# A transformer block on one core: the place of some products, copies, maxima and one feed-forward half in a written-out order of tasks

## The chip, the cores and the metric

The kernel runs on one core of a Trainium2 chip. The metric is the device time of one execution in microseconds (us), as the median of three runs. One more execution was recorded by the profiler. A core has these engines, each of which runs its own queue of instructions in order: TensorE (PE, with its weight loads shown apart as PEld), VectorE (DVE), ScalarE (ACT), GpSimd (POOL) and SyncE (SP), which here only starts transfers. An instruction waits until the instructions that it depends on, on whatever engine, are done, and everything behind it on its own engine waits too.

## The reference

The input x has 8 batches of 512 tokens with 128 features. Everything is float32. The computation has three steps:

```python
x = x + 0.5 * ffn(layernorm(x))
x = x + attn(layernorm(x))
x = x + 0.5 * ffn(layernorm(x))
```

```python
# ffn: three blocks, each with two quantized linear layers with a low-rank addition
h = x
for blk in range(3):
    y = qlora_linear(h, 2 * blk)
    y = gelu(layernorm(y) * gamma[blk] + beta[blk])     # exact Gelu
    h = qlora_linear(y, 2 * blk + 1) + h
# attn: 16 heads of rank 64
xq = einsum('btd,hrd->bthr', x, Q)
xk = einsum('bud,hrd->buhr', x, K)
scores = einsum('bthr,buhr->bthu', xq, xk) / sqrt(128)
out = einsum('bthu,bud,hde->bte', softmax(scores), x, VO)
```

## The kernel before

**Attention.** The heads are taken two at a time, so a batch has 8 pairs and the program 64. A pair is laid out over a period of 16 units of an abstract time, that is two halves of 8 units. In each half two of the four chunks of 128 query rows are treated: PE makes the scores of both heads (`scores`, L554), DVE their negated maxima (`maxima`, L570), ACT the exponentials with their sums (`exps`, L573), DVE the inverse of the sums (`inverse`), POOL and ACT the divisions (`divide`, L585: one head on POOL, the other on ACT, or both on POOL in halves listed in `gelu_halves`). DVE transposes blocks of 32 by 32 (`turn`, L592), and 16 transfers started on SP move the blocks between groups of partitions (`exchange`, L603). One period later PE multiplies the result with the values (`attend`, L620, one 512-column product for each head and chunk, summed in one PSUM bank over the 8 pairs of a batch). In the first half of a pair PE also makes the projections of the next pair (`project`, L507) and in the second half the values (`values`, L534), which ACT copies.

**Feed-forward.** One half of the feed-forward (first or last, f = 0 or 1) of one batch is laid out by `lay_ffn` (L449) as a unit in the midst of the attention, up to two units at a time. A unit normalizes its input, and then has three blocks of four halves each: first product (L278), bias and statistics on DVE (L286), root on POOL, scaling on DVE, transpose on PE, Gelu on ACT (L303, with a load of ACT's function table before it and one for the exponentials after it), second product (L312) and sum on DVE (L318). A last transpose and sum go back to x (`ffn_add`, L328). Batch 0's first and batch 7's last feed-forward are laid out by `lay_parts` (L409) at the start and the end of the program, in two parts of 256 tokens each, where nothing runs beside them but the weights' preparation.

**Order.** `at(t, fn, *args)` notes a task with its time. At the end `run_tasks` sorts all tasks by time and then by the order of noting, and calls them. The times are not waited for: they only fix the order of the instructions on each engine, which is kept by dependencies between neighbours. So a change of a time matters where it passes another task with work on the same engine.

**The start.** Abstract time starts at T0 = -33; pair 0 has its first scores at 0. Before that lie the weights' preparation (`Weights`, two groups of layers), the transposes of Q and K by `projection_weights` (L219), each with a copy by ACT, and batch 0's first feed-forward. In halves 0 to 3 no attention products can run yet: this is called the filling. In it, `busy` puts transposes of nothing on PE.

Of the kernel before, what the change touches and what calls it, by code (L numbers as in the profile page):

```python
# [18 lines left out]
def kernel(  # L19
# [25 lines left out]
    nc = tc.nc  # L45
# [8 lines left out]
    NC = T // P  # L54
# [3 lines left out]
    HALF = 8.0  # L58
# [9 lines left out]
    def bank(name, tag="proj"):  # L68
        return psum.tile([P, NC, P], F32, tag=tag, name=name, bufs=1)

    ident = const.tile([P, P], F32, name="ident")
# [57 lines left out]
    def at(t, fn, *args):  # L129
        tasks.append((t, len(tasks), fn, args))  # L130
# [44 lines left out]
    class Weights:  # L175
# [33 lines left out]
        def turn(self):  # L209
            pt = bank(f"pt_w{self.l0}", "proj")  # L210
            for l in range(self.n):
                nc.tensor.transpose(pt[:, l, :], wf[:, self.l0 + l, :], ident)
            nc.scalar.copy(wT[:, self.l0 : self.l1, :], pt[:, : self.n, :])
# [2 lines left out]
    qT_w = const.tile([P, HP, P], F32, name="qT_w")  # L216
    kT_w = const.tile([P, HP, P], F32, name="kT_w")

    def projection_weights(src, dst, g0, scale, nm):  # L219
        pt = bank(f"pt_{nm}{g0}", "proj")  # L220
        for j in range(NC):
            nc.tensor.transpose(pt[:, j, :], src[:, g0 + j, :], ident)
        nc.scalar.mul(dst[:, g0 : g0 + NC, :], pt, scale)

    def transposed(src, name, tag):

# [219 lines left out]

    gelu_halves = set()

    def lay_ffn(units, t0, lead=None):  # L449

        for i, unit in enumerate(units):
            if unit is None:
                continue
            f, b = unit  # L460
            tag = f"f{i}"
            n = Norm(xs[b], f"n{f}_{b}", tag)
            t = t0 + i * HALF
            for at_n, (fn, *args) in zip(
                lead or [t + 6.0] + [t + HALF + dt for dt in (0.5, 2.6, 4.2, 6.5)],
                ((n.stats,), (n.root,), (n.scale,), (n.turn,), (ffn_start, n, f, b)),
            ):
                at(at_n, fn, *args)
            for k in range(NB):
                u = t0 + (2 + 4 * k) * HALF  # L470
                t = u + i * HALF
                m = Block(f, k, b, tag)
                gelu_halves.add(round((u + 2 * HALF) / HALF))
                at(t + 2.3, m.first)
                at(t + 6.0, m.biased)
                at(t + HALF + 0.5, m.root)
                at(u + 2 * HALF + 2.6, m.scale)
                at(u + 2 * HALF + 4.2 + i, m.turn)
                at(u + 2 * HALF + 6.5, m.gelu)
                at(u + 3 * HALF + 2.3 + 1.9 * i, m.second)  # L480
                at(u + 3 * HALF + 6.0, m.add)
            at(t0 + (2 + 4 * NB) * HALF + 2.3 + 1.9 * i, ffn_add, f, b, tag)

# [146 lines left out]
    def attn_add(b):  # L630
        oT = work.tile([P, NC, P], F32, tag="oT", name=f"oT{b}", bufs=2)
        nc.vector.tensor_copy(
            oT.rearrange("p c (i q) -> p i c q", q=32),
            accs[b].rearrange("p (i c q) -> p i c q", i=Q4, q=32),
        )

        def turn():
            po = transposed(oT, f"pot{b}", "f0")
            nc.vector.tensor_tensor(xs[b], xs[b], po, ALU.add)

        return turn
# [18 lines left out]
    def lay_pair(n, b, g):  # L660

        m = Pair(b, g)
        t = n * PERIOD
        if n == 0:
            for i in range(2):
                for (wt, nm), tm, tag in zip(  # L670
                    ((kT_w, "k"), (qT_w, "q")), ((-3.6, -3.5), (-1.1, 0.3))[i],
                    (("proj", "f0"), ("proj", "f1"))[i],
                ):
                    at(tm, m.project_part, wt, nm, i, tag)
        else:
            for i, (wt, nm) in enumerate(((qT_w, "q"), (kT_w, "k"))):
                at(t - PERIOD + 2.5 + 2.7 * i, m.project, wt, nm)
                at(t - PERIOD + 3.9 + 2.3 * i, m.keep, nm)
        for c in range(NC):
            h, i = c // 2, c % 2  # L680
            u = t + h * HALF
            at(u, m.scores, c)
            at(u + 1.2 + 1.3 * i, m.maxima, c)
            at(u + 2.6 + 1.5 * i, m.exps, c)
            at(u + 4.4 + 1.2 * i, m.inverse, c)
            at(u + 4.5 + 1.2 * i, m.divide, c, 0, "pool")
            shared = "pool" if 2 * n + h in gelu_halves else "act"
            at(u + 5.0 + 0.75 * i, m.divide, c, 1, shared)
            at(u + (HALF + 2.7 if i else 6.9), m.turn, c)
        at(t + PERIOD + 2.8, m.exchange)  # L690
        for i in range(2):
            u = t + PERIOD + HALF
            at(u - HALF + 2.4 if m.last else u + 2.5 + 2.7 * i, m.values, 2 * i)
            at(u - HALF + 2.5 if m.last else u + 3.9 + 2.3 * i, m.keep_values, 2 * i)
        for i in range(2 * NC):
            u = t + 2 * PERIOD + i // NC * HALF
            at(u + (3.0, 3.5, 4.0, 5.0)[i % NC], m.attend, i // NC, i % NC)
        if g == HP - 1 and b < B - 1:
            done = []
            at(t + 3 * PERIOD - 0.1, lambda: done.append(attn_add(b)))  # L700
            at(t + 3 * PERIOD + 4.2, lambda: done[0]())
# [5 lines left out]
    T0 = -33.0  # L707
# [3 lines left out]
    at(T0 + 6.0, busy, 4)  # L711
    at(T0 + 9.65, columns)
    for (l0, l1), times in zip(groups, (
        (5.4, 5.5, 6.1, 6.55, 7.3, 7.8), (8.3, 9.0, 10.0, 10.6, 11.9, 12.65)
    )):
        m = Weights(l0, l1)
        for t, fn in zip(
            times, (m.dequantized, m.lora_turn, m.lora_keep, m.lora, m.add, m.turn)
        ):
            at(T0 + t, fn)  # L720
    for t, (src, dst, g0, scale, nm) in zip((17.55, 20.35, 23.05, 26.0), (
        (q_sb, qT_w, 0, 1.0 / math.sqrt(D), "q"), (k_sb, kT_w, 0, 1.0, "k"),
        (q_sb, qT_w, NC, 1.0 / math.sqrt(D), "q"), (k_sb, kT_w, NC, 1.0, "k"),
    )):
        at(T0 + t, projection_weights, src, dst, g0, scale, nm)

    def input_part(m, t):
        def keep():
# [11 lines left out]
        0, 0, [[T0 + t for t in times] for times in (  # L740
            (3.7, 6.4, 7.2, 7.6, 7.5), (4.3, 7.7, 8.2, 8.6, 9.6)
        )],
        T0 + 8.7, 1.4, (2, 2, 2), input_part,
    )
    at(T0 + 27.3, table, AF.Exp)
    for t in (26.6, 28.0, 29.9, 30.8):
# [1 line left out]
    for h in range(4):  # L748
        at((h + 1) * HALF - 0.1, busy, 12)

    lay_ffn([(0, 1)], -2 * HALF, (-3.3, -2.9, -1.6, 0.5, 0.6))
    lay_ffn([None, (0, 2)], 6 * HALF)
    for b in range(B):
        t = b * HP * PERIOD
        if b + 1 < B:
            lay_attn_input(b + 1, t + (4 if b else 12) * HALF)
        if b:
            halves = [(1, b - 1)]
            if b + 2 < B:
                halves.append((0, b + 2))  # L760
            lay_ffn(halves, t + 5 * HALF)
    for n in range(B * HP):
        lay_pair(n, n // HP, n % HP)


    E = (B * HP + 2) * PERIOD

    def store_part(m, t):
# [8 lines left out]
        1, B - 1, [[E + t for t in times] for times in (  # L777
            (1.8, 3.7, 4.2, 4.6, 1.5), (2.8, 4.8, 5.3, 5.7, 1.6)
        )],
        E + 5.0, 1.1, (6, 6, 6), store_part,  # L780
    )
    at(E + 1.65, idle_bank, "acc")
    at(E + 1.7, busy, 18)
# [54 lines left out]
```

## Time and profile before

| | before |
|---|---|
| median of three runs | 1152.51 us (1152.16 to 1153.66) |
| profiled execution | 1156.43 us |
| its span, first to last instruction | 1154.6 us |
| granted TensorE clock, mean | 0.996 |
| PE, DVE, ACT, POOL busy | 96%, 75%, 64%, 50% of the span |
| 16 transfers of each exchange (`eT<-tr`) | 128 KB each, 2.3 us from issue to landing (median) |

A row of the timeline gives start, duration, engine, line, operation, what is written and read, the count, and in brackets the idle time of the engine before it and what ended it. `L314` is line 314 of the kernel. A row of a wait list gives the total in us, the number of times and the longest. A matmul in float32 shows as two records. Small differences between rows come from records that overlap.

### The profile page before, as it was taken

The page shows a single profiled execution, that of the slowest core. Times are in us where ns is not written, and L with a number is a line of the kernel's source. Part 1 is how long each engine was busy: PE and PEld are TensorE (multiplying, and loading weights), DVE is VectorE, ACT ScalarE, POOL GpSimd, SP SyncE. Part 2 cuts the span into 40 slices and gives each one's busy share as a digit, 9 for nine tenths or more (in the row PEclk, how much of TensorE's full clock was granted, in tenths as well). Part 3 has the DMA queues.
Part 4 walks back from the last instruction along what each step waited for, and adds up shares of the span by engine and source line. Part 5 has one row for each costly group of instructions (what it writes and reads, how often), then busy time and mean ns, then how long its engine had stood idle before and what let it go on. Part 6 is the DMA issues. An engine that isn't in the chain of part 4 may idle for free.

```text
span 1154.6 us, 14081 instructions
## 1 busy us (share of the span) xinstructions
PE 1106.9 (96%) x3951; PEld 553.3 (48%) x3951; DVE 862.7 (75%) x1771; ACT 743.0 (64%) x1632; POOL 572.7 (50%) x477
## 2 busy tenths in 40 slices
PE   8789999999999999999999999999999999999997
PEld 6444444445444444444444444444444444444445
DVE  5667777887879777887778787797778777677635
ACT  2567676766666766767666666676666676766731
POOL 2345555554546455455545546454554555545512
PEclk9989999999999999999999999999999999999999
DMA  6055565566546545654655564565465656655550
GB/s 175 1 121 112 132 137 128 112 134 147 117 112 147 130 107 128 142 130 110 139 117 125 133 141 106 128 146 119 107 139 131 139 114 137 150 134 123 129 141 10
DMA packets 57286, 142.29 MB, mean 123 GB/s; under 512 B 18348, under 2 KB 22008, under 8 KB 57208
## 3 DMA queue, kind: packets, MB, share of 16 engines
q1 hardware_dynamic: 54840, 139.73, 53.9%
q10 hardware_dynamic: 2368, 1.66, 0.6%
q8 instruction: 32, 0.52, 0.2%
q14 instruction: 46, 0.38, 0.1%
HBM read 5.01 MB, written 2.10 MB: 6 GB/s over the span
## 4 chain that ended last, share of the span: by engine, by line
PE 84%; ACT 7%; DVE 4%; SPq 2%; DMA 1%; issue 1%; POOL 1%; ACTq 0%; DVEq 0%
PE acc L624 36%; PE ps L564 16%; PE pv L544 9%; PE pq L510 5%; PE pk L510 4%; PE py L281 4%; PE po L314 4%; ACT L306 3%; SPq L613 2%; ACT aT L306 2%; PE p L230 2%; DVE tr L598 1%; ACT v L550 1%; DVE nm L571 1%; DMA eT<-tr 1%
## 5 line engine op out<-in xcount | busy, mean ns | idle before, releaser
L588 POOL TENSOR_SCALAR e<-e,rden 128x512 f32<-128x512 f32 x306 | 476.1, 1568 | 510.0 <-DVE rden L583 510.0
L576 ACT ACTIVATE e<-ps,nm 128x512 f32<-128x512 f32 x512 | 349.5, 692 | 197.6 <-DVE nm L571 195.3
L624 PE MATMUL acc<-eT,v 128*128 128x512 f32 x1024 | 471.6, 593 | 3.2 <-DMA eT<-tr 1.7
L598 DVE STREAM_TRANSPOSE tr<-e 128x1024 f32<-128x1024 f32 x256 | 315.6, 1233 | 107.4 <-POOL e L588 103.3
L571 DVE TENSOR_REDUCE nm<-ps 128x2 f32<-128x1024 f32 x256 | 299.3, 1206 | 18.9 <-PE ps L564 17.5
L624 PEld LDWEIGHTS acc<-eT,v 128*128 128x128 f32 x1024 | 189.9, 190 | 200.3 <-issue 189.5
L564 PE MATMUL ps<-k,q 64*128 64x512 f32 x1024 | 254.9, 616 | 1.9 <-ACT e L576 1.5
L564 PEld LDWEIGHTS ps<-k,q 64*128 64x128 f32 x1024 | 88.2, 186 | 130.1 <-issue 79.2
L590 ACT ACTIVATE e<-e,rden 128x512 f32<-128x512 f32 x206 | 138.2, 728 | 7.1 <-DVE rden L583 6.8
L544 PE MATMUL pv<-vo_sb,axT 128*128 128x256 f32 x512 | 135.6, 388 | 4.4 <-ACT v L550 4.4
L550 ACT COPY v<-pv 128x512 f32<-128x512 f32 x128 | 74.6, 583 | 76.3 <-PE pv L544 75.9
L583 DVE RECIPROCAL rden<-den 128x2 f32<-128x2 f32 x256 | 36.0, 148 | 113.2 <-ACT e L576 111.9
L544 PEld LDWEIGHTS pv<-vo_sb,axT 128*128 128x128 f32 x512 | 91.6, 191 | 58.8 <-issue 35.6
L576 ACT ACTIVATION_READ_ACCUMULATOR e<-ps,nm 128x1 f32 x512 | 105.6, 206 | 0.0
L510 PE MATMUL pq<-axT,qT_w 128*128 128x512 f32 x126 | 67.0, 613 | 0.0
L510 PE MATMUL pk<-axT,kT_w 128*128 128x512 f32 x126 | 64.5, 593 | 0.7 <-ACT q L516 0.7
L314 PE MATMUL po<-aT,wT 128*128 128x512 f32 x84 | 45.4, 622 | 19.4 <-ACT aT L306 19.4
L516 ACT COPY k<-pk 128x512 f32<-128x512 f32 x63 | 37.2, 591 | 35.0 <-PE pk L510 34.7
L281 PEld LDWEIGHTS py<-wT,hT 128*128 128x128 f32 x336 | 40.7, 191 | 32.0 <-ACT hT L326 10.8
L281 PE MATMUL py<-wT,hT 128*128 128x128 f32 x336 | 48.7, 288 | 0.7 <-ACT hT L326 0.7
L576 ACT ACT_TABLE_LOAD x25 | 32.1, 1283 | 24.1 <-DVE nm L571 24.1
L254 POOL TENSOR_TENSOR rstd<-rstd,mhalf 128x4 f32<-128x4 f32 x42 | 43.6, 1038 | 3.5
(99 smaller groups left out, 722.2 us busy)
## 6 DMA issues: line engine op xcount, KB each, us to landing
eT<-tr SPq DMA_DIRECT2D x1016, 128.0 KB, 2.3
x<-in_L_attn_x_dram SPq DMA_DIRECT2D x8, 256.0 KB, 5.6
out_dram<-x SPq DMA_DIRECT2D x7, 256.0 KB, 2.4
eT<-tr ACTq DMA_DIRECT2D x8, 128.0 KB, 3.6
qk_sb<-in_L_attn_Q_dram SPq DMA_DIRECT2D x1, 512.0 KB, 4.5
qk_sb<-in_L_attn_K_dram SPq DMA_DIRECT2D x1, 512.0 KB, 5.8
q_i<-in_L_ffn_qweights_dram ACTq DMA_DIRECT2D x1, 256.0 KB, 5.0
out_dram<-x SPq DMA_DIRECT2D x2, 128.0 KB, 1.7
```

The source lines that it names most:

```text
L281: nc.tensor.matmul(self.py[:, c, :], lhsT=hTs[self.b][:, c, :], rhs=wT[:, 2 * self.k, :], start=True, stop=True,)
L314: nc.tensor.matmul(self.po, lhsT=wT[:, 2 * self.k + 1, :], rhs=self.aT, start=True, stop=True)
L510: nc.tensor.matmul(self.pg, lhsT=wt[:, self.g, :], rhs=xTs[self.b], start=True, stop=True)
L544: nc.tensor.matmul(self.pv[:, 2 * c : 2 * c + 2, :], lhsT=xTs[self.b][:, c0 + c, :], rhs=vo_sb[:, 2 * self.g : 2 * self.g + 2, :], start=T ...
L550: nc.scalar.copy(self.v[:, c0 : c0 + 2, :, :].rearrange("p c h d -> p (c h) d"), self.pvs[c0])
L564: nc.tensor.matmul(ps[:, j, :], lhsT=self.q[rows, ts(c, P)], rhs=self.k[rows, :], start=True, stop=True,)
L571: nc.vector.tensor_reduce(self.nm[:, c, :], self.ps[c], AX.X, ALU.max, negate=True)
L576: nc.scalar.activation(e[:, j, :], self.ps[c][:, j, :], AF.Exp, bias=self.nm[:, c, j : j + 1], accum_out=self.den[:, c, j : j + 1],)
L588: nc.gpsimd.tensor_scalar(e, e, r, None, ALU.mult)
L590: nc.scalar.activation(e, e, AF.Copy, scale=r)
L598: nc.vector.transpose(self.tr[:, :, :, c, :], self.e[c].rearrange("p h (k j r) -> p j (h k) r", j=Q4, r=32),)
L624: nc.tensor.matmul(accs[self.b], lhsT=self.v[:, k, j, :], rhs=self.eT[:, :, j * NC + k, :], start=(self.g == 0 and j == 0 and k == 0), sto ...
```

## The change

- `projection_weights` notes two tasks, one for the transposes on PE and one for the copy on ACT, with a time for each.
- `lay_ffn` takes the times of the input's normalization for each unit. The second unit's are given for the filling.
- The second product of the first unit goes from 2.3 to 3.2 in its half, the second unit's stays at 4.2. The projection or the first values are at 2.5 and the four attention products at 3.0, 3.5, 4.0 and 5.0.
- For pairs 0 and 1 the transposes of the even chunks go from 6.9 to behind the maxima of the next half (2.5 there).
- In the second group of weights a product and a sum go behind other tasks.
- Both calls of `lay_parts` get another distance between the two parts in the first block (1.4 to 2.55 at the start, 1.1 to 1.4 at the end).
- The first feed-forward of batch 2 is laid beside that of batch 1, from the beginning of the filling, instead of from half 6.

```diff
-    def projection_weights(src, dst, g0, scale, nm):
-        pt = bank(f"pt_{nm}{g0}", "proj")
-        for j in range(NC):
-            nc.tensor.transpose(pt[:, j, :], src[:, g0 + j, :], ident)
-        nc.scalar.mul(dst[:, g0 : g0 + NC, :], pt, scale)
+    def projection_weights(src, dst, g0, scale, nm, t, t_keep):
+        def turn():
+            pt = bank(f"pt_{nm}{g0}", "proj")
+            for j in range(NC):
+                nc.tensor.transpose(pt[:, j, :], src[:, g0 + j, :], ident)
+            at_keep.append(pt)
+
+        at_keep = []
+        at(t, turn)
+        at(t_keep, lambda: nc.scalar.mul(dst[:, g0 : g0 + NC, :], at_keep[0], scale))
...
-    def lay_ffn(units, t0, lead=None):
+    def lay_ffn(units, t0, lead={}):
...
-                lead or [t + 6.0] + [t + HALF + dt for dt in (0.5, 2.6, 4.2, 6.5)],
+                lead.get(i) or [t + 6.0] + [t + HALF + dt for dt in (0.5, 2.6, 4.2, 6.5)],
...
-                at(u + 3 * HALF + 2.3 + 1.9 * i, m.second)
+                at(u + 3 * HALF + 3.2 + i, m.second)
...
-            at(u + (HALF + 2.7 if i else 6.9), m.turn, c)
+
+            at(u + (HALF + 2.7 if i else 6.9 if n > 1 else HALF + 2.6), m.turn, c)
...
-        (5.4, 5.5, 6.1, 6.55, 7.3, 7.8), (8.3, 9.0, 10.0, 10.6, 11.9, 12.65)
+        (5.4, 5.5, 6.1, 6.55, 7.3, 7.8), (8.3, 9.0, 10.0, 11.4, 12.5, 12.65)
...
-    for t, (src, dst, g0, scale, nm) in zip((17.55, 20.35, 23.05, 26.0), (
+    for (t, t_keep), (src, dst, g0, scale, nm) in zip((
+        (17.55, 18.0), (20.0, 20.4), (23.05, 23.4), (26.0, 26.1)
+    ), (
...
-        at(T0 + t, projection_weights, src, dst, g0, scale, nm)
+        projection_weights(src, dst, g0, scale, nm, T0 + t, T0 + t_keep)
...
-        T0 + 8.7, 1.4, (2, 2, 2), input_part,
+        T0 + 8.7, 2.55, (2, 2, 2), input_part,
...
-    lay_ffn([(0, 1)], -2 * HALF, (-3.3, -2.9, -1.6, 0.5, 0.6))
-    lay_ffn([None, (0, 2)], 6 * HALF)
+    lay_ffn([(0, 1), (0, 2)], -2 * HALF, {
+        0: (-3.3, -2.9, -1.6, 0.5, 0.6), 1: (-1.5, -1.4, 2.6, 4.2, 6.5)
+    })
...
-        E + 5.0, 1.1, (6, 6, 6), store_part,
+        E + 5.0, 1.4, (6, 6, 6), store_part,
```

## The prediction

> **What bounds the kernel now.** I read the page first, then TensorE's waits, then the timeline of one four-half cycle of feed-forward, then VectorE's rows in the same cycle, then the start and the end.
>
> ```profile
> PE 1106.9 (96%) x3951; PEld 553.3 (48%) x3951; DVE 862.7 (75%) x1771; ACT 743.0 (64%) x1632; POOL 572.7 (50%) x477
> ...
> PE 84%; ACT 7%; DVE 4%; SPq 2%; DMA 1%; issue 1%; POOL 1%; ACTq 0%; DVEq 0%
> ```
>
> TensorE (PE) carries the end. Its largest wait has one cause:
>
> ```profile
> PE po L314 <- ACT aT L306: 19.4, 23, 1.0
> ```
>
> Every one is the first unit's second product (L314): scores end, Gelu is not ready, 22 times 0.84 us and once 1.03. A cycle in the timeline:
>
> ```profile
> 523.55 1.99 PE L564 MATMUL ps<-k,q 64*128 64x512 f32 x8
> ...
> 525.55 1.45 ACT L306 ACTIVATE aT<-p,cols 128x512 f32<-128x512 f32 x2
> 526.38 1.13 PE L314 MATMUL po<-aT,wT 128*128 128x512 f32 x2 [0.84 <-ACT aT L306]
> ...
> 527.34 1.02 PE L510 MATMUL pq<-axT,qT_w 128*128 128x512 f32 x2
> ...
> 528.20 2.74 PE L624 MATMUL acc<-eT,v 128*128 128x512 f32 x6
> ```
>
> The projection and the attention products behind the wait had their data. But VectorE (DVE) is close behind. One cycle of it:
>
> ```profile
> 550.95 2.35 DVE L571 TENSOR_REDUCE nm<-ps 128x2 f32<-128x1024 f32 x2
> 553.22 2.13 DVE L259 TENSOR_SCALAR z<-y,mv,rstd 128x128 f32<-128x128 f32 x8
> ...
> 559.80 1.25 DVE L598 STREAM_TRANSPOSE tr<-e 128x1024 f32<-128x1024 f32 x1 [3.19 <-POOL e L588]
> 560.97 2.32 DVE L571 TENSOR_REDUCE nm<-ps 128x2 f32<-128x1024 f32 x2
> ```
>
> From maxima to maxima the chain DVE, ACT, POOL, DVE needs 10.02 us here, whatever PE does.
>
> **What the Trainium skill says.** "ScalarE: Activation LUTs", What ACT_TABLE_LOAD costs: about 1283 ns a load, the same for every set; the trace agrees (32.1 us for 25 loads, 1283 mean). "TensorE: Matmul & The Clock Gate", What's actually happening: after some 3.4 us idle the array runs at half clock. The trace agrees: after a 3.77 us gap at 64.8, 12 idle transposes took 2.77 us (1.47 elsewhere). "Perfetto Trace Analysis", Optimization Strategy: with several regimes, the most contended engine changes over time; so it is here, so I count by stage.
>
> **Second products later.** Of 42 blocks the 24 of the first unit move; the other unit's keep their place between the third and fourth attention product. I number halves from the first scores (0). In a Gelu half (the scores after a Gelu) the new order is scores, projection (or values), one attention product, second product. A 512-column product costs 0.857 us (3.43 for four in the chain of waits), a projection the same. Gelu ends 2.8 us after the scores start (its table load follows the copy of the values, which waits for PE just before the scores). The product now comes at 1.92 + 0.86 + 0.86 = 3.64 us: no wait. PE's halves in a two-unit cycle become 8.17 + 8.16 + 8.15 + 9.05 = 33.53 instead of 34.37.
> The DVE chain's own times between maxima are 10.02 (above), 8.44 (526.60 to 535.04), 7.75 and 8.16, the last two less 0.14 and 0.06 that DVE waits for PE by its own back-to-back step (1.17 from transpose to maxima): 7.61 + 8.10. Sum 34.17. So DVE falls behind PE by 0.64 us a cycle. Let L be maxima start minus scores start (minimum 1.17, when PE decides). Halves 56 to 72, one batch, start with L = 1.18; then by chain minus PE period: 1.18, 3.05, 2.44, 1.88, 1.82, 3.69, 3.08, 2.52, 2.46. There z (ready L + 3.45 after scores) is later than its transpose at 5.46: PE waits 0.45. After the third cycle L is about 3.4. The exchange lands 15.97 us after these maxima (477.77 to 493.74 in another batch), the next pair's attention product stands at 15.42 + 2.82 = 18.24 after the scores: wait 3.4 + 16.0 - 18.2 = 1.2, against about 0.3 now. In a batch PE thus saves 3 x 0.84 = 2.5 and gives back 0.45 + 0.9, leaving 1.1; DVE's 0.8 waits (two in a batch, at the last sum and the first maxima after) are the slack this uses. Five batches (halves 24 to 104): 5.0 us, between 0 and 12.6.
> In the last two batches only one unit runs; PE has 8.17 + 7.27 + 7.71 + 9.03, DVE waits for PE 0.33 + 0.72 in each cycle, more than 0.84. Four Gelus gain 0.84, less 0.15 each because attention products, now 2.78 us after the scores instead of 4.5, come to within 0.3 us of the landing of their exchange: 2.8 us.
> In the drain, the last transfers are issued at 1114.48 and land about 1117.1, where the attention products start; the second product (1115.65) lay in that gap and now stands behind the first of them: it loses 0.86, I take -0.8. The fifth Gelu gains nothing (maxima to maxima 7.28, DVE's chain).
>
> **Copies of Q and K behind Gelu.** Now:
>
> ```profile
> 19.74 0.60 ACT L223 ACTIVATE qT_w<-pt_q 128x512 f32<-128x512 f32 x1 [3.58 <-PE pt_q L222]
> 20.24 0.56 ACT L384 ACTIVATE aT<-p_b,cols 128x256 f32<-128x256 f32 x1
> ...
> 26.53 0.60 ACT L223 ACTIVATE qT_w<-pt_q 128x512 f32<-128x512 f32 x1 [2.04 <-PE pt_q L222]
> 27.02 0.56 ACT L384 ACTIVATE aT<-p_b,cols 128x256 f32<-128x256 f32 x1
> ```
>
> Gelu stood behind a copy that waited for PE. The larger lag (1.4 to 2.55) delays the second part's first block by up to 1.7 us, to 18.35 for its next product against 17.73, which pushes the first part's transpose from 18.62 to 19.05. Followed step by step with these durations: Gelu 19.55 (was 20.24), second product 20.2 (20.85), third Gelu 25.5 (27.02), second 26.15 (27.63), last Gelu 28.5 (29.97). First scores 36.5 instead of 37.92: 1.4 us. The later products and sum of the second weight group end at 13.7 as now, because the first block's normalization (11.65 to 13.05) takes their place, not an idle gap. No DMA or POOL work is added. Bounds: 0.7, if the second part's delay takes more of it, and 2.0, if both parts reach their 5.5 us step.
>
> **Filling.** Batch 2's first feed-forward block moves from halves 8 to 11 into 1 to 3, and maxima go ahead of transposes. In old time:
>
> ```profile
> 62.84 1.25 DVE L598 STREAM_TRANSPOSE tr<-e 128x1024 f32<-128x1024 f32 x1 [3.02 <-POOL e L588]
> 64.00 2.31 DVE L571 TENSOR_REDUCE nm<-ps 128x2 f32<-128x1024 f32 x2
> ...
> 74.58 2.35 DVE L571 TENSOR_REDUCE nm<-ps 128x2 f32<-128x1024 f32 x2 [2.72 <-PE ps L564]
> ```
>
> Maxima by half, worked with the same durations: half 1, 47.9 (48.68); half 2, 54.7 (55.06: a transpose and a 1.0 wait leave, 1.9 of bias and statistics enters); half 3, 63.7 (64.00: bound by the new transposes of x2, the k projection and twelve idle ones); there the transpose now waits for POOL (to 68.1) with the reciprocals behind it, and ACT's divisions behind those. But the values, which waited 3.77 us for a copy, follow at 68.3, and the next maxima at 71.7 with a warm clock or 73.0 with a cold one: 2.2 us gained of 74.58. The statistics of x2 (1.2 us of DVE) go into an idle 1.97 before the first maxima, its root (0.23 + 1.04) into idle POOL time; no transfer is added, and the first exchange (transpose end 61.45, landing 73.7) meets its product at about 74.6; were it later, the attention products and the block's second product would queue behind it on PE. Bounds: 1.6 and 2.9.
> Then halves 4 to 24, now 163.8 us: gone from PE are one block (8 products and 4 transposes, 0.9 + 0.43, and 0.86), 2.2; the input's and last transposes that go along, 0.4; two Gelu waits, 1.7; a cold 1.2 in half 4; an issue gap 0.7. Sum 6.2, given back: DVE's 0.64 twice, and in 7.27 us halves the exchange's tight landing, 0.6. 4.3 us net. POOL gets two fewer halves of all-POOL divisions.
>
> **Tail.** With 1.4 the first part's next product no longer stands behind the second part's transpose, product and bias (0.8 us of PE at 1135.65 to 1136.43). Gain 0.9; nothing if the second part's own chain, 0.3 later by order, sets the end.
>
> **Sum.** 1.4 + 2.2 + 4.3 + 5.0 + 2.8 - 0.8 + 0.9 = 15.8. Span 1154.6 to 1138.8; that execution took 1156.43, 3.9 above the median of the runs, 1152.51. From the median: 1136.7 us.
>
> **Rivals.** (1) PE keeps everything: DVE's chain has slack I have not seen (a 0.23 wait before the transposes of even halves may go). For: DVE is 75% busy. Against: its intervals repeat to 0.02. Then 7.5 more: 1129. (2) DVE's chain eats the gain in the batches and the filling stays cold: 5.0 + 1.3 + 1.4 less: 1144. For: 34.17 against 34.37. (3) Slower: attention products, now ahead of the second product, meet an exchange that has not landed, and everything waits behind. Landing in a cycle is about 16.4 after maxima (511.99, last issue 521.93, 2.3 to land), the product stands at 19.1: slack 1.5 to 1.6 at L = 1.18, 0.8 at 1.88. It decides if the stall exceeds my sum by 15.8 / 23 = 0.7 us in each Gelu half, so L 1.5 above mine; at twice that, 1168. (4) Nothing changes, were Gelu late by 1.7 us more: excluded by its fixed 2.8.
>
> **Chances.** Forecast 0.52 (own range 1132 to 1141), (1) 0.15, (2) 0.22, (3) 0.08, no change 0.03. The range 1129 to 1147 takes in (1)'s and (2)'s centres with the unknown costs and leaves about 0.2 out. Faster by over 0.2% 0.89, within 0.2% 0.03 (what this measurement cannot tell from none), slower 0.08.
>
> **What would show it.** No TensorE wait on Gelu at L314 but the last. Waits on z at L230 and on eT at L624 instead, some 1 us a batch. Gelu ahead of L223. First scores near 36.5, half 4's near 70. Two fewer Gelu halves (table loads at L576 25 to 23). Wrong if eT waits exceed 15 us or L314's wait stays.

## The result and the profile after

| | before | changed |
|---|---|---|
| median | 1153.09 us (1152.16 to 1154.99, 4 runs) | 1137.27 us (1135.74 to 1138.69, 4 runs) |
| profiled execution | 1156.43 us | 1135.74 us |
| its span | 1154.6 us | 1133.9 us |

The ratio of the times is 0.986, with a 95% interval of 0.9839 to 0.9882. The changed kernel is 15.8 us faster. The two profiled executions differ by 20.7 us, because the one of before was 3.3 us above its median and the changed one 1.5 us below. The four runs of the changed kernel lie in two pairs, 1135.74 and 1135.90 us at a mean granted clock of 0.996 and 1138.63 and 1138.69 us at 0.992, and the median falls between them. A comparison of both kernels on another chip gave 0.9835 (0.9821 to 0.9849), 18.8 us.

In the changed kernel lines 224 to 688 have moved by five: scores are L569, maxima L576, exponentials L581, divisions L593 (POOL) and L595 (ACT), transposes L603, attention products L629, second products L319, Gelu L311, projections L515. Its page has, for the engines' busy time and for the chain that ended last:

```profile
PE 1109.9 (98%) x3951; PEld 552.2 (49%) x3951; DVE 859.0 (76%) x1771; ACT 738.4 (65%) x1632; POOL 565.9 (50%) x473
...
PE 82%; DVE 7%; SPq 3%; ACT 3%; POOL 2%; DMA 2%; issue 1%; ACTq 0%; DVEq 0%
```

PE has the same number of instructions and is busy for 98% of a shorter span. DVE's part of the chain has grown from 4 to 7%. PE's waits in the changed kernel (total, times, longest):

```profile
PE acc L629 <- DMA eT<-tr: 4.5, 4, 3.3
PE p L235 <- DVE z L264: 2.8, 1, 2.8
...
PE pk L515 <- ACT q L521: 1.2, 6, 0.2
```

The 19.4 us at the second product are gone, all 23. Waits for transfers came up to 4.5 us, of which 3.3 are one wait near the end. A small new row, the k projection behind ACT's copy of q, will matter below. PE's timeline in a Gelu half of the changed kernel:

```profile
544.22 1.99 PE L569 MATMUL ps<-k,q 64*128 64x512 f32 x8
546.13 1.13 PE L515 MATMUL pq<-axT,qT_w 128*128 128x512 f32 x2
547.10 1.02 PE L629 MATMUL acc<-eT,v 128*128 128x512 f32 x2
547.96 1.02 PE L319 MATMUL po<-aT,wT 128*128 128x512 f32 x2
```

The projection and one attention product fill the time in which Gelu runs. The next rows are DVE's timeline around the same half:

```profile
537.75 2.32 DVE L576 TENSOR_REDUCE nm<-ps 128x2 f32<-128x1024 f32 x2
539.99 2.12 DVE L264 TENSOR_SCALAR z<-y,mv,rstd 128x128 f32<-128x128 f32 x8
...
546.56 1.25 DVE L603 STREAM_TRANSPOSE tr<-e 128x1024 f32<-128x1024 f32 x1 [3.19 <-POOL e L593]
547.73 2.32 DVE L576 TENSOR_REDUCE nm<-ps 128x2 f32<-128x1024 f32 x2
```

From maxima to maxima DVE still needs 9.98 us here (10.02 before), and the same 3.19 us wait for POOL. The maxima start 3.51 us behind the scores, where before they started 3.05 us behind. This distance is the prediction's L.

To see where the time went I cut the program at the start of the scores of halves 0, 4, 24, 104 and 127 (us, from two traces of each kernel):

| stretch | before | before, again | changed | changed, again | forecast gain | gain, pair 1 / pair 2 |
|---|---|---|---|---|---|---|
| start, to half 0 | 37.92 | 38.04 | 35.85 | 36.57 | 1.4 | 2.1 / 1.5 |
| filling, 0 to 4 | 35.21 | 33.01 | 33.08 | 31.98 | 2.2 | 2.1 / 1.0 |
| 4 to 24 | 163.77 | 163.09 | 159.04 | 159.40 | 4.3 | 4.7 / 3.7 |
| five two-unit batches, 24 to 104 | 675.32 | 675.74 | 665.64 | 666.20 | 5.0 | 9.7 / 9.5 |
| last batches, 104 to 127 | 182.87 | 181.98 | 178.05 | 177.83 | 2.8 | 4.8 / 4.2 |
| drain and tail | 59.51 | 60.04 | 62.24 | 62.52 | 0.1 | -2.7 / -2.5 |

The drain is what follows the scores of half 127 up to the last sum of attention, the tail the rest. The gains of the two pairs add up to 20.7 and 17.4 us. So the sum came out nearly as forecast and four of its terms did not: the batches and the last batches gained more, the filling in the second pair less, and the drain lost more. The start as the changed kernel has it, on ACT:

```profile
24.94 0.56 ACT L389 ACTIVATE aT<-p_b,cols 128x256 f32<-128x256 f32 x1 [1.91 <-PE p_b L235]
25.41 0.59 ACT L228 ACTIVATE qT_w<-pt_q 128x512 f32<-128x512 f32 x1
```

Gelu is now first, the copy behind it. Gelu runs at 24.94 where 25.5 was forecast, and the first scores come at 35.85 (36.57 in the second trace) where 36.5 was forecast.

### The profile page after: what moved, and what is told of

It reads as the page before. It is cut to its first block, busy times and chain, and to the rows that moved or that the text cites. A ratio compares the mean times of both kernels' runs of the same rounds, so it can differ in the third digit from the quotient of the medians.

```text
span 1133.9 us, 14061 instructions
## 1 busy us (share of the span) xinstructions
PE 1109.9 (98%) x3951; PEld 552.2 (49%) x3951; DVE 859.0 (76%) x1771; ACT 738.4 (65%) x1632; POOL 565.9 (50%) x473
## 4 chain that ended last, share of the span: by engine, by line
PE 82%; DVE 7%; SPq 3%; ACT 3%; POOL 2%; DMA 2%; issue 1%; ACTq 0%; DVEq 0%
PE acc L629 33%; PE ps L569 19%; PE pv L549 9%; PE pk L515 5%; PE pq L515 5%; PE py L286 4%; SPq L618 3%; PE po L319 2%; DVE nm L576 2%; DVE tr L603 2%; POOL e L593 2%; PE p L235 1%; DMA eT<-tr 1%; PE warm_acc L149 1%; ACT e L581 1%
## 5 line engine op out<-in xcount | busy, mean ns | idle before, releaser
L593 POOL TENSOR_SCALAR e<-e,rden 128x512 f32<-128x512 f32 x302 | 469.8, 1567 | 494.5 <-DVE rden L588 494.5
L581 ACT ACTIVATE e<-ps,nm 128x512 f32<-128x512 f32 x512 | 350.0, 694 | 214.7 <-DVE nm L576 213.1
L629 PE MATMUL acc<-eT,v 128*128 128x512 f32 x1024 | 476.8, 594 | 5.0 <-DMA eT<-tr 4.5
L603 DVE STREAM_TRANSPOSE tr<-e 128x1024 f32<-128x1024 f32 x256 | 315.8, 1235 | 101.3 <-POOL e L593 98.8
L576 DVE TENSOR_REDUCE nm<-ps 128x2 f32<-128x1024 f32 x256 | 298.4, 1203 | 16.1 <-PE ps L569 15.7
L629 PEld LDWEIGHTS acc<-eT,v 128*128 128x128 f32 x1024 | 189.8, 190 | 204.1 <-issue 193.0
L569 PE MATMUL ps<-k,q 64*128 64x512 f32 x1024 | 254.8, 615 | 1.0 <-ACT e L581 0.5
L569 PEld LDWEIGHTS ps<-k,q 64*128 64x128 f32 x1024 | 87.9, 186 | 129.0 <-issue 91.2
L595 ACT ACTIVATE e<-e,rden 128x512 f32<-128x512 f32 x210 | 141.3, 731 | 3.2 <-DVE rden L588 3.0
L581 ACT ACTIVATION_READ_ACCUMULATOR e<-ps,nm 128x1 f32 x512 | 106.4, 208 | 0.0
L515 PE MATMUL pq<-axT,qT_w 128*128 128x512 f32 x126 | 69.0, 629 | 0.0
L515 PE MATMUL pk<-axT,kT_w 128*128 128x512 f32 x126 | 66.2, 607 | 1.2 <-ACT q L521 1.2
L264 DVE TENSOR_SCALAR z<-y,mv,rstd 128x128 f32<-128x128 f32 x168 | 44.9, 344 | 0.0
```

The costliest lines, as they stand in the source:

```text
L264: nc.vector.tensor_scalar(z[:, c, :], self.src[:, c, :], self.mv[:, c, 0:1], self.rstd[:, c : c + 1], ALU.subtract, ALU.mult,)
L515: nc.tensor.matmul(self.pg, lhsT=wt[:, self.g, :], rhs=xTs[self.b], start=True, stop=True)
L569: nc.tensor.matmul(ps[:, j, :], lhsT=self.q[rows, ts(c, P)], rhs=self.k[rows, :], start=True, stop=True,)
L576: nc.vector.tensor_reduce(self.nm[:, c, :], self.ps[c], AX.X, ALU.max, negate=True)
L581: nc.scalar.activation(e[:, j, :], self.ps[c][:, j, :], AF.Exp, bias=self.nm[:, c, j : j + 1], accum_out=self.den[:, c, j : j + 1],)
L593: nc.gpsimd.tensor_scalar(e, e, r, None, ALU.mult)
```

## The experiments

Times are ratios to the kernel before on the same chip, with 95% intervals; microseconds are medians (before: 1155.04 in the first eight runs, which fell on two chips, and 1155.21 in the last four, on a third). The last four are one_act, before_again, only_second and only_start.

**What the later second products are worth.** One kernel is the changed one unaltered; one puts the second product back where it was; one puts it between the two, behind the projection but ahead of the first attention product.

undo_second:

```diff
-                at(u + 3 * HALF + 3.2 + i, m.second)
+                at(u + 3 * HALF + 2.3 + 1.9 * i, m.second)
```

second_one:

```diff
-                at(u + 3 * HALF + 3.2 + i, m.second)
+                at(u + 3 * HALF + 2.6 + 1.6 * i, m.second)
```

> The changed kernel once more, as the measure of the other three on the same chip. Theory A (the forecast's: after the change VectorE's chain of maxima, exponentials, divisions and transposes sets the pace of the two-unit batches, with TensorE waiting on it in Gelu halves and at the exchange) and theory B (TensorE alone sets the pace, what is left of its waits is independent of the chain) both say 1136 to 1139 us, span 1133.9 or 1136.8.

> The changed kernel with the second products back at 2.3 and 4.2, everything else as changed. The forecast's sum gives 7 us more than the changed kernel (5.0 + 2.8 - 0.8). The two traces by stage give more: 9.7 in halves 24 to 104, 4.3 after, 1.7 for two Gelu halves early, less about 2 in the drain: 13 to 14 us, so 1150 to 1151. If the gain of the stages came mostly from the other edits, under 3. TensorE's wait on Gelu comes back: 0.84 in each first-unit Gelu half.

> The first unit's second product behind the projection (or values) only, ahead of all four attention products (2.6 in place of 3.2). Theory: one product of 0.86 us covers the 0.84 us that Gelu is late, so the cycles stay as they are (Gelu halves 8.98), and in the drain the product no longer stands behind the attention product that waits 3.3 us for its transfer: 1 to 3 us less than the changed kernel. Rival: it takes two products to cover Gelu, then a wait of 0.1 to 0.4 us in each of 21 Gelu halves comes back, 2 to 8 us more.

Measured: the changed kernel 0.9835 (0.9821 to 0.9849), 1136.22 us; undo_second 0.9943 (0.9929 to 0.9957), 1148.48; second_one 0.982 (0.9805 to 0.9835), 1134.10. The later second products are worth 12.3 us in the changed kernel, where the prediction has at most 8.7 (5.0 + 2.8 - 0.8, and 1.7 for the two Gelu waits between halves 4 and 24, from which it takes a part back). With the old place, PE's list of waits has the old row again:

```profile
PE po L319 <- ACT aT L311: 19.4, 23, 1.0
```

The place behind the projection alone is as good: its interval overlaps with that of the changed kernel, so the 2.1 us between the two are not settled.

**Is it DVE's chain that holds the batches?** If the chain DVE, ACT, POOL, DVE limits PE in the batches, shortening it must give time, though no engine loses work. The chain passes POOL because both heads of a Gelu half are divided there. This kernel gives the first chunk's second head back to ACT in these halves:

```diff
-            shared = "pool" if 2 * n + h in gelu_halves else "act"
+            shared = "pool" if i and 2 * n + h in gelu_halves else "act"
```

> The changed kernel, but in halves where POOL did all four divisions, the second head of the even chunk is divided on ScalarE again: the transpose behind it waits for one POOL operation (1.56 us) in place of two (3.1). Theory A: the 10.0 us interval of the chain falls to 8.5, its sum is under TensorE's 33.5, the lag goes back to 1.2 in each cycle, and the Gelu halves of 9.13 and 9.45 us and the wait at the exchange fall to the first one's 8.98: 3 to 6 us less than the changed kernel. Theory B: no change, or up to 2 us more for the extra work on ScalarE (24 divisions of 0.73 us).

Measured: 0.9786 (0.977 to 0.9801), 1130.52 us, 5.7 faster than the changed kernel. DVE's timeline around the same Gelu half:

```profile
535.80 2.36 DVE L576 TENSOR_REDUCE nm<-ps 128x2 f32<-128x1024 f32 x2
538.07 2.13 DVE L264 TENSOR_SCALAR z<-y,mv,rstd 128x128 f32<-128x128 f32 x8
...
543.10 1.25 DVE L603 STREAM_TRANSPOSE tr<-e 128x1024 f32<-128x1024 f32 x1 [1.64 <-POOL e L593]
544.27 2.32 DVE L576 TENSOR_REDUCE nm<-ps 128x2 f32<-128x1024 f32 x2
```

The wait for POOL fell from 3.19 to 1.64 and maxima to maxima from 9.98 to 8.47. PE's halves and L in halves 58 to 68, from the starts of scores and maxima in three traces:

| half | 58 | 59 | 60 | 61 | 62 | 63 | 64 | 65 | 66 | 67 | 68 |
|---|---|---|---|---|---|---|---|---|---|---|---|
| before: us | 9.89 | 8.17 | 8.16 | 8.15 | 9.89 | 8.17 | 8.16 | 8.15 | 9.89 | 8.10 | 7.71 |
| changed: us | 8.98 | 8.17 | 8.16 | 8.15 | 9.13 | 8.16 | 8.16 | 8.16 | 9.44 | 8.11 | 7.92 |
| chain_act: us | 8.98 | 8.17 | 8.16 | 8.15 | 8.99 | 8.16 | 8.16 | 8.16 | 8.98 | 8.10 | 7.71 |
| before: L | 3.05 | 1.60 | 1.18 | 1.18 | 3.05 | 1.59 | 1.17 | 1.26 | 3.09 | 1.63 | 2.59 |
| changed: L | 3.04 | 2.50 | 1.91 | 1.68 | 3.51 | 2.82 | 2.23 | 2.00 | 3.83 | 2.82 | 2.86 |
| chain_act: L | 1.50 | 1.64 | 1.18 | 1.18 | 1.50 | 1.63 | 1.18 | 1.18 | 1.49 | 1.63 | 2.58 |

In the changed kernel L grows from cycle to cycle and the Gelu halves with it, from 8.98 to 9.13 and 9.44. With the shorter chain L falls back to 1.18 in each cycle and every Gelu half stays at 8.98 or 8.99. The five batches take 662.25 us in this trace, 3.4 and 4.0 us less than in the two traces of the changed kernel, and halves 4 to 24 take 158.08, which is 1.0 and 1.3 less. That DVE's chain took part of the gain in the changed kernel is thus shown, with its size.

**Both together.** The chain of chain_act and the place of second_one:

```diff
-                at(u + 3 * HALF + 3.2 + i, m.second)
+                at(u + 3 * HALF + 2.6 + 1.6 * i, m.second)
-            shared = "pool" if 2 * n + h in gelu_halves else "act"
+            shared = "pool" if i and 2 * n + h in gelu_halves else "act"
```

> The two edits of the earlier runs together: the first unit's second product behind one product only, and the even chunk's second division on ScalarE in Gelu halves. If they act on different things (the drain, the chain), they add: 5.7 and 2.1 us less than the changed kernel, 1128 to 1129 us. If the shorter chain already takes away what the earlier product gains, as chain_act alone, 1130 to 1131.

Measured: 0.978 (0.9767 to 0.9792), 1130.31 us. That is not told apart from chain_act. Both beat the kernel before and the changed one.

**The other parts, taken back one at a time.**

undo_fill gives batch 2's first unit and the transposes of the filling their old places:

```diff
-            at(u + (HALF + 2.7 if i else 6.9 if n > 1 else HALF + 2.6), m.turn, c)
+            at(u + (HALF + 2.7 if i else 6.9), m.turn, c)
-    lay_ffn([(0, 1), (0, 2)], -2 * HALF, {
-        0: (-3.3, -2.9, -1.6, 0.5, 0.6), 1: (-1.5, -1.4, 2.6, 4.2, 6.5)
-    })
+    lay_ffn([(0, 1)], -2 * HALF, {0: (-3.3, -2.9, -1.6, 0.5, 0.6)})
+    lay_ffn([None, (0, 2)], 6 * HALF)
```

undo_turns has only the first of these two edits. undo_copies puts each copy directly behind its transposes, at the old times (the transposes of the second pair, moved from 20.35 to 20.0 by the change, go back too):

```diff
-        (17.55, 18.0), (20.0, 20.4), (23.05, 23.4), (26.0, 26.1)
+        (17.55, 17.55), (20.35, 20.35), (23.05, 23.05), (26.0, 26.0)
```

undo_lags gives both calls of `lay_parts` the old distance between the two parts (the lag), and the second group of weights its old times:

```diff
-        (5.4, 5.5, 6.1, 6.55, 7.3, 7.8), (8.3, 9.0, 10.0, 11.4, 12.5, 12.65)
+        (5.4, 5.5, 6.1, 6.55, 7.3, 7.8), (8.3, 9.0, 10.0, 10.6, 11.9, 12.65)
-        T0 + 8.7, 2.55, (2, 2, 2), input_part,
+        T0 + 8.7, 1.4, (2, 2, 2), input_part,
-        E + 5.0, 1.4, (6, 6, 6), store_part,
+        E + 5.0, 1.1, (6, 6, 6), store_part,
```

> The changed kernel with batch 2's first feed-forward back in halves 6 to 20 and the transposes of the first two pairs back at 6.9, everything else as changed. The forecast gave the two edits 2.2 us in the filling and, without the Gelu waits, some 2.6 to 3.4 in halves 4 to 24: 5 to 6 us more than the changed kernel (1141 to 1142). If the moved block only shifts the load into the filling, which ScalarE, VectorE and POOL bound, 0 to 2.

> The changed kernel with only the transposes of the first two pairs back at 6.9, ahead of the next half's maxima. If the order matters, the maxima of halves 1 to 4 come 1.2 us later each time a transpose stands ahead of them or waits for POOL there: 1 to 3 us more than the changed kernel, seen in the scores of half 4. If TensorE's idle time in the filling has another cause (a half-rate clock, the projection behind the transposes), 0.

> The changed kernel with the copies of Q's and K's transposes at the transposes' own old times again, so ahead of Gelu, and the rest as changed. By the forecast's steps Gelu stood behind such a copy for about 0.7 us in the second block and 0.8 more in the third: first scores 1 to 1.7 us later (37.2 to 37.9), the whole 1 to 1.7 us more. If the weights or VectorE set the pace of the start, 0.

> The changed kernel with the distances of the two parts back (1.4 at the start, 1.1 at the end) and the second weight group's product and sum back. The forecast has the end gain 0.9 from its edit and the start lose up to 0.4 from its own (a part's transpose behind the other part's product): 0.5 to 1 us more than the changed kernel, the end 1 us longer after the last sum of attention and the first scores at the same time or up to 0.4 earlier. Rival: the parts in step with each other make the start's gain, then first scores 1 us later or more.

| | ratio | us | above the changed | first scores | half 0 to 4 | 4 to 24 | drain and tail |
|---|---|---|---|---|---|---|---|
| changed, again | 0.9835 | 1136.22 | | 36.57 | 31.98 | 159.40 | 62.52 |
| undo_fill | 0.9882 (0.9865 to 0.9899) | 1141.58 | 5.4 | 36.04 | 33.01 | 161.96 | 63.74 |
| undo_turns | 0.9846 (0.9831 to 0.9861) | 1137.55 | 1.3 | 35.93 | 34.70 | 159.35 | 62.75 |
| undo_copies | 0.9852 (0.9831 to 0.9873) | 1138.16 | 1.9 | 37.66 | 32.40 | 159.69 | 60.53 |
| undo_lags | 0.9847 (0.983 to 0.9864) | 1138.15 | 1.9 | 36.02 | 32.48 | 160.07 | 63.35 |

Only undo_fill stands clear of the changed kernel; the intervals of the other three overlap with it. The stretches say more. The place of the copies moves the first scores (37.66 with the old one; 37.92 and 38.04 in the kernel before), and the start's larger lag does not move them (36.02 without it). The filling's edits pay after the filling: with batch 2's unit back in halves 8 to 11, halves 4 to 24 take 161.96 instead of 159.0 to 159.4. Inside the filling undo_fill's 33.01 is no slower than the 33.08 in one trace of the changed kernel, and 1.0 slower than the 31.98 in the other. By a single trace the order of maxima and transposes, with the second unit there, is worth 1.6 to 2.7 in the filling (34.70 against 33.08 and 31.98); the 1.3 us of its medians are not clear of noise. The shorter tail shows from the sum of the last attention (`oT`) to the end: 28.9 to 29.2 us with the new lag, 29.9 to 30.0 with the old one, in every trace.

**One part at a time on the kernel before.**

before_again is the kernel before, unaltered. only_second has the edit of the second products and nothing else:

```diff
-                at(u + 3 * HALF + 2.3 + 1.9 * i, m.second)
+                at(u + 3 * HALF + 3.2 + i, m.second)
```

only_start has the start's edits and nothing else, with the change to `projection_weights` itself:

```diff
-        (5.4, 5.5, 6.1, 6.55, 7.3, 7.8), (8.3, 9.0, 10.0, 10.6, 11.9, 12.65)
+        (5.4, 5.5, 6.1, 6.55, 7.3, 7.8), (8.3, 9.0, 10.0, 11.4, 12.5, 12.65)
...
-    for t, (src, dst, g0, scale, nm) in zip((17.55, 20.35, 23.05, 26.0), (
+    for (t, t_keep), (src, dst, g0, scale, nm) in zip((
+        (17.55, 18.0), (20.0, 20.4), (23.05, 23.4), (26.0, 26.1)
+    ), (
...
-        T0 + 8.7, 1.4, (2, 2, 2), input_part,
+        T0 + 8.7, 2.55, (2, 2, 2), input_part,
```

> The kernel before, once more with a profile. In its first trace the four halves of the filling took 35.2 us, and 33.0 in the changed kernel with the filling undone. If the 2.2 us belong to the order of the work, 35.2 again; if they belong to where TensorE's half-rate clock fell (68 to 75 us in the first trace, 54 to 60 in the changed kernel's), 33 to 35.5, and not twice the same.

> The kernel before with the second products later and nothing else. If this edit's gain does not depend on the others: 11 to 13 us less than before, most of it in halves 24 to 127, with the drain 1 to 3 us longer. If it needs the other edits (the filling's shift), under 8.

> The kernel before with the start's edits alone (copies behind Gelu, the parts 2.55 apart, the second weight group's product and sum later): first scores at 36.0 to 36.6, 1.4 to 2 us less than before. The filling from first scores to half 4's: 35.2 if order decides it, since its order is that of before, 33 to 34 if the clock does.

Measured: before_again 1153.74 us (one execution); only_second 0.9902 (0.9885 to 0.9919), 1143.68; only_start 0.9995 (0.9986 to 1.0004), 1153.87. The second products alone give 11.5 us: in their trace against that of before, 8.2 in the batches, 5.0 in the last ones, 1.1 from 4 to 24, less 3.9 in drain and tail. The start alone gives nothing that can be measured, though its first scores came at 36.06 instead of 37.92. Its filling took 34.62 us, and the same unchanged filling took 35.21 and 33.01 in the two traces of before. TensorE's granted clock was at half rate for a few us in each of these traces. Stretches of the filling in the first trace of before (columns: stretch, its length, busy PE, PEld, DVE, ACT, POOL, granted clock of TensorE, transfers' share, GB/s):

```profile
68.00:76.00 8.00, 7.44 (x30) 5.35 (x31) 3.55 (x6) 3.66 (x10) 3.13 (x2) 0.64 0.34 75
```

and in before_again:

```profile
52.00:60.00 8.00, 5.03 (x16) 1.99 (x13) 6.35 (x13) 5.30 (x15) 3.30 (x3) 0.84 0.00 1
```

The same kernel runs at reduced clock at 68 to 76 in the one and at 52 to 60 in the other, where 68 to 76 is then at full clock. In the first case it falls on the values and the scores of half 4, for which everything behind them waits. Five traces have the filling in this order (undo_fill and only_second too, but for the place of one second product). They sort by the half-rate stretches, read from the clock in narrow windows: 35.21 and 35.21 us with one from 66.9 (66.7 in only_second) to 73.7 (73.5), 34.62 with one at 57.1 to 60.5 and one at 67.3 to 70.7, 33.01 and 33.01 with one that ends by 61. So the 2.2 us go with the place of the half rate and not with the order of the work.

**The drain.** From the end of the last transpose on DVE to the sum of the last attention, over all fourteen traces, by two circumstances: where the fifth Gelu's second product stands, and whether a half-rate stretch shows behind the last transfers.

| second product | full clock | half rate |
|---|---|---|
| ahead of the attention product | 18.40 (before), 18.90 (before_again), 18.96 (only_start), 19.21 (one_act) | 20.55 (undo_second), 20.63 (second_one) |
| behind it | 19.57 (undo_copies) | 21.36 (changed), 21.35 (changed, again), 21.48 (only_second), 21.45 (chain_act), 21.40 (undo_lags), 21.54 (undo_turns); 22.56 (undo_fill, half rate for twice as long) |

The means are 18.87 and 20.59 above, 19.57 and, without undo_fill, 21.43 below: the order costs 0.7 to 0.8, the half rate 1.7 to 1.9. Each stretch but undo_fill's is 3.41 us long, so at half rate it can cost 1.7 us at most where PE alone decides. The 19.57 stands on one trace, and the four above it spread by 0.8, so the price of the order rests mainly on the half-rate column. PE's timeline in the changed kernel:

```profile
1095.07 2.05 PE L629 MATMUL acc<-eT,v 128*128 128x512 f32 x2 [3.29 <-DMA eT<-tr]
1096.91 1.61 PE L319 MATMUL po<-aT,wT 128*128 128x512 f32 x2
```

A product that takes 1.02 elsewhere takes 2.05. In undo_copies, with a gap of 2.90 at the same place:

```profile
1096.48 1.10 PE L629 MATMUL acc<-eT,v 128*128 128x512 f32 x2 [2.90 <-DMA eT<-tr]
1097.42 1.02 PE L319 MATMUL po<-aT,wT 128*128 128x512 f32 x2
```

And with the second product ahead, in second_one:

```profile
1093.59 1.12 PE L319 MATMUL po<-aT,wT 128*128 128x512 f32 x2 [1.13 <-ACT aT L311]
1095.68 5.37 PE L629 MATMUL acc<-eT,v 128*128 128x512 f32 x8 [0.96 <-DMA eT<-tr]
```

Here the same eight records take 5.37 us that took 3.67 in the trace of before. So putting the product ahead saves its 0.8 and does not by itself keep the clock.

What sets the half rate in the drain can be read from the clock that `--windows` gives. In each trace the granted clock is 1.00 or 0.50 and changes only at multiples of 3.413 us from one of its changes to the next (in the changed kernel at 57.02 and at 1094.67, 304 such steps apart). Cut into these steps, undo_copies has, around its gap from 1093.58 to 1096.48,

```profile
1091.38:1094.80 3.42, 2.21 (x9) 0.85 (x7) 0.00 (x0) 2.06 (x2) 0.00 (x0) 1.00 1.05 231
1094.80:1098.21 3.41, 1.73 (x4) 0.87 (x5) 0.00 (x0) 0.00 (x0) 0.00 (x0) 1.00 0.14 30
```

and chain_act, with a gap of 2.90 too, from 1087.02 to 1089.92:

```profile
1087.29:1090.70 3.41, 0.78 (x2) 0.49 (x3) 0.00 (x0) 0.60 (x1) 0.00 (x0) 1.00 0.43 94
1090.70:1094.12 3.42, 3.42 (x5) 1.35 (x4) 0.75 (x1) 0.00 (x0) 0.00 (x0) 0.50 0.00 0
```

In undo_copies an edge divides the gap, PE is busy for 2.21 and 1.73 us of the two steps, and the clock stays. In chain_act 2.63 us of the gap lie in one step, PE is busy for 0.78 us of it, and the next step runs at half rate. In the drains of the fourteen traces all nine steps ahead of a half rate have PE busy for 0.28 to 1.64 us, and every other full-rate step for 1.73 or more.

## Why the prediction was right, and where its steps were not

The sum was 15.8 and so is the difference of the medians (18.8 on the other chip). One of its sums has a slip: 2.5 less 0.45 and 0.9 leaves 1.1 a batch, which is 5.5 us for five batches, not 5.0. By stretches, against the second pair of traces, its terms missed by +0.1, -1.2, -0.6, +4.5, +1.4 and -2.6, which add up to 1.6. The total was right partly by luck, because errors of both signs met.

**Gelu is in time.** Right: the product comes 3.74 us after the scores in the half shown (3.64 forecast), its wait's 23 occurrences are gone from PE's list, and undo_second brings them back.

**Two-unit batches: 5.0 forecast, 9.5 to 9.7 measured.** The mechanism was right and chain_act shows it; the size was off. By the table of halves a batch saves 0.91 + 0.76 + 0.45 in its Gelu halves and gives back 0.21 in half 68, which is 1.9 instead of 1.1. The mis-sized term was DVE's cycle, 34.17. It measures 33.93 (maxima at 513.80 and at 547.73, halves 58 and 62): of its intervals 9.98 was forecast as 10.02, 7.93 as 8.10. PE's cycle is 33.46, forecast as 33.53. So the first cycle loses 0.50 and the second, in which PE's Gelu half is longer by 0.15, 0.32, where 0.64 was forecast for each. L in half 65 is then 2.00, where 2.46 was forecast. The wait for z, 0.45, needs L above 5.46 - 3.45 = 2.01; it never came. The wait for the exchange at a batch's end was forecast as 1.2 against 0.3, which is 4.5 us more in five batches. By the lengths of halves 38, 54 and 70 over the 7.70 of 86 and 102, which do not wait, it was 1.48 and 2.65 us in all in the two traces of the changed kernel and 1.93 and 2.32 in those of before, so no more was given back there than two traces of one kernel differ by. What was given back came by a way that I had not listed: exponentials late by L hold ACT's copy of q behind them, and the k projection on PE, at the end of a Gelu half, waits for that copy (the row of 1.2 us in six waits above, and the halves of 9.13 and 9.44). The row is less than the halves lose, since it counts from the modelled end of the product before. With the shorter chain of chain_act that row is 0.2 us in one wait. In all, a batch gives back 0.8 of a possible 2.7 us (three times 0.91), where 1.35 of 2.5 was forecast.

**Last batches: 2.8 forecast, 4.2 to 4.8 measured.** The 0.15 given back at each Gelu did not come: three of the four Gelu halves fell from 9.03 to 8.12 and one to 8.20, 3.6 us in all. Another 0.5 is half 126, which fell from 7.31 to 6.80 and for which nothing was forecast; the drain gives it back (below).

**Start: 1.4 forecast, 1.5 to 2.1 measured.** Right, and by the copies, as worked (undo_copies). Of the first pair's 2.1, 0.36 is there already at PE's first product (8.68 instead of 9.04), before any edit acts. That the lag delays the second part's first block did not matter, and without it nothing was lost.

**Filling: 2.2 forecast, 1.0 to 2.1 measured, and the reason given was not the right one.** Half 4 starts at 68.93 us, as forecast (near 70), and one feed-forward block more is done by then. But the unchanged filling takes 33.0 or 35.2 us, by the place of its half-rate stretch. I took the slower as the kernel's own time and put its difference down to the edits; what the edits bring is a block that costs nothing there. The cold stretch itself was misread too: the prediction has it follow the 3.77 us gap at 64.8, but the clock was at half rate from 66.89 on, 2.1 us into that gap. From **4 to 24**, where that unit is missing, 4.3 was forecast and 3.7 to 4.7 measured, and undo_fill gives 2.6 to 2.9 of it back. Of what the forecast counted, 1.2 was the half rate in half 4, which only the first trace of before has.

**Drain: -0.8 forecast, -3.7 and -3.2 measured (29.6 and 30.1 us before, 33.3 in both traces of the changed kernel); tail: 0.9 forecast, 0.8 to 1.0 measured.** The 0.8 for the second product behind the attention product agrees with the table of the drain. Two terms were missing: the half-rate stretch, 1.8, and 0.8 for the last transposes, which end 12.0 us after the scores of half 127 instead of 11.2, since DVE's chain is late by L to the end (the maxima of half 127 at 3.21 behind the scores, 2.42 before).

**The rivals.** (1), PE keeps everything, came half true: the batches got 9.5 of 12.6 us. Its 1129 is what chain_act reaches (1130.5), once the chain is shorter. (2) fell: the chain did not eat the batches, and the filling was not slower than before. (3) fell: waits for transfers are 4.5 us in all against 1.7. (4) fell, since 12.3 us go with the edit.

"TensorE: Matmul & The Clock Gate", What's actually happening, of the Trainium skill says that the windows over which activity is judged run free of the program. The traces agree: the steps of 3.413 us in the drain's section lie differently against the program in each trace (the half rate of the filling begins at 57.02 and at 55.22 in the two of the changed kernel), and the same gap of 2.90 us is followed by full clock in undo_copies and by half rate in chain_act (attention product 1.28, second product 1.91). What stays open is the exact measure: in the filling thirteen of fifteen steps ahead of a half rate have PE busy for at most 1.59 us, but two have 2.12 (changed) and 2.41 (undo_second), and one of 1.62 (undo_second) was followed by full clock.

## What to carry to other kernels

A wait at the head of the busiest engine's queue is worth its length only as far as the next engine's chain can follow: here PE's cycle of 33.5 us came under a chain of 33.9 through engines that were busy for 76, 65 and 50%, so measure from one instance of an instruction to its next one before counting the gain, and look for the part of the chain that can change engines (5.7 us here for one division moved). Before an edit is credited with a gain in a sparsely filled stretch, compare two traces of the unchanged kernel: 2.2 us of a filling of 35 were not the edit's. A product that moves behind a wait for a transfer costs its own length where the engine has nothing else to do (0.8 us in the drain).

## What the runs showed that I had not expected

- Half-rate stretches follow groups of short gaps. In undo_second and second_one the gaps ahead of the eight slow records (5.37 us instead of 3.67) were 0.98 and 0.86, and 1.13 and 0.96; each pair lay in one step of 3.413 us (but for 0.3 us in second_one), of which PE was busy for 1.58 and 1.64 us. In only_start gaps of 1.23 and 0.89 lay in two steps, with PE busy for 2.44 and 2.26, and were followed by full clock. The prediction took from "TensorE: Matmul & The Clock Gate", What's actually happening, that some 3.4 us of idle time are needed; here a step that was idle for about half of its length was enough, and the measurement decides.
- A single placement of a division (one of two heads of one chunk, from POOL to ACT, in 23 halves) took 1.5 us out of a chain of 10 us and L from 3.05 to 1.50, although POOL was busy for half of the span only.
